# Eleven late tiles' second FFNs held back instead of eight, and the products of the last norms on VectorE

## The chip, the cores and the metric

One core of one Trainium2 chip. The metric is device time in microseconds (us) of one launch. In the text, TensorE is the matmul engine (PE in the profile, PEld its weight loads), VectorE is DVE, ScalarE is ACT, GpSimd is POOL, and SP is the engine that issues nearly all DMAs. Each engine runs its instructions in the order in which the program gives them; semaphores hold an instruction until what it needs is there.

## The reference: what is computed

The input x has 4 batches of 4096 rows of 512 numbers (f32). One block of a network is computed:

```
x = x + 0.5 * ffn(layernorm(x))
x = x + attention(layernorm(x))        # 16 heads of 32, each row sees 13 neighbours
x = x + 0.5 * ffn(layernorm(x))        # the same weights as above
```

`ffn` is one 512 x 512 matrix product in which both sides are first quantised in blocks of 32 numbers: block maximum of the absolute values divided by 7.5 is the scale, the quotient is rounded to a grid of 6-bit floats, and the result is multiplied back. The attention is local: 13 neighbours with a bias for each relative position, softmax, then a 512 x 512 projection.

## The kernel before

**Tiles and precision.** The 16384 rows are 128 tiles (NT) of 128 rows. All large products are made of f16 high and low halves: `product` (L146) issues twelve matmuls of 128x128 on 128x512 (low by high, high by low, high by high, over four chunks of 512), all recorded on L151. A tile needs six such products in some form: the first FFN, the values, its share of the q and k projections (made for four tiles together, two products for each of four chunks of heads), the output projection and the second FFN.

**The schedule.** The work is software-pipelined by hand. `begin(slot, stage, rank)` (L162) puts a generator into a numbered slot; `run_slot` (L165) runs the stages of a slot by rank, and a stage that yields `(n, rank)` goes on n slots later with that rank. The order in which the slots emit instructions is the order on each engine. A tile, and an item of attention (one chunk of four heads for four tiles; there are 128 items m), takes STEP = 7 slots. For tile t with k = 7t: load at k - 18, first norm at k - 10, first FFN at k + 5, values at k + 20, output projection at `out_slot(t)`, usually k + 93, second FFN at `second_slot(t)`, usually 12 slots after the output projection. For item m with k = 7m: q and k projections at k + 38 and k + 39, scores (`softmax`, line L442 on TensorE, into `ps`) at k + 42, probabilities by values (`attend`, L512, into `pv`) at k + 59.

**A quantised norm.** `quantised_norms(slot)` (L220) makes the quantised input of an FFN, for all tiles that `enlist` put into this slot. In the middle of the kernel these are two: the third norm n3 of tile t (before its second FFN), and the first norm n1 of tile t + 15, because 7t + 95 is the slot of both; each instruction then works on 1024 columns. Its stages, mostly one slot apart: `factors` (L183; GpSimd: variance to reciprocal root, L186, L189, L192), normalising (ScalarE, L233), block maxima, scale and reciprocal (VectorE, L239, L240, L244), product with the reciprocal (GpSimd, L246), rounding to fp8 (ScalarE, L249), product with the scale (GpSimd, L251), high half (ScalarE, `high`, L200), low half (VectorE, `low`, L204) and the DMA transpose by SP (L205) into `xT`, the left side of the FFN. The fp8 tile has one buffer (pool `q8p`, L99), as has the f16 tile of the halves (pool `hlp`, L100). `spare` (L227) is true when the first tile of a norm is 123 or later; then y and the halves lie in buffers of the pool `xp` (L96, 23 buffers, which hold the rows of the tiles in flight).

**Between scores and scores.** For item m: VectorE adds the bias and the two parts of the scores (L467, L470) and takes the maximum `top` (L474); GpSimd subtracts it (L476); ScalarE takes exp (L478); VectorE sums and inverts (`total`, L481 to L483); GpSimd multiplies (L485); ScalarE makes the f16 copies (L489, L490); GpSimd the low part (L492); SP transposes p (L494). The q and k of the next item are evacuated between: high halves by ScalarE (L373), low halves by VectorE (L377); the scores of the item wait for the second low half. `ring` (L539 and L545) holds the attention's output.

**The end.** Tiles 113 to 120 are `HELD` (L582): their second FFN waits for the end of the pipeline. Their `xT` takes a buffer of `xp`. `second_slot` (L595) spreads them over slots 932 to 946, among the output projections of 121 and 122 and the last `attend`s (pv 125 at slot 934, pv 126 at 941, pv 127 at 948). Then come the output projections of 123 to 127 (slots 951 to 959), the second FFNs of 121 and 122 (960, 961) and of 123 to 127 (963 to 971). The values of the last group of items are brought back from DRAM as stacks (L418), issued by SP among its transposes and stores (L564). The bias of a second FFN is added on GpSimd (L573).

The lines that place the held tiles:

```
HELD = range(NT - 15, NT - 7)
...
if t in HELD:
    return (n_items - 1) * STEP + PV - (16, 13, 10, 6, 5, 4, 3, 2)[t - HELD[0]]
if i in (-2, -1):
    return out_slot(NT - 1) + 3 + i
return out_slot(t) + F2
```

Of the kernel before, what the change touches and what calls it, by code (L numbers as in the profile page):

```python
# [27 lines left out]
F16 = mybir.dt.float16  # L28
# [4 lines left out]
ALU = mybir.AluOpType  # L33
# [4 lines left out]
P = 128  # L38
# [7 lines left out]
GROUP = 4  # L46
# [4 lines left out]
QB = 32  # L51
# [13 lines left out]
def macaron_kernel(  # L65
# [12 lines left out]
    nc = tc.nc  # L78
# [3 lines left out]
    KC = dim // P  # L82
# [3 lines left out]
    NT = n_batch * length // P  # L86
# [15 lines left out]
    x2p = ctx.enter_context(tc.tile_pool(name="x2p", bufs=2))  # L102
# [26 lines left out]
    def bc(t, n):  # L129

        return t.unsqueeze(2).to_broadcast([t.shape[0], t.shape[1], n])
# [14 lines left out]
    def product(pm, lhs, rhs):  # L146

        n = 0
        for a, b in ((0, 1), (1, 0), (0, 0)):
            for c in range(KC):  # L150
                nc.tensor.matmul(  # L151
                    pm, lhs(a, c), rhs(b, c), start=(n == 0), stop=(n == 3 * KC - 1)
                )
                n += 1
# [7 lines left out]
    def begin(slot, stage, rank=5):  # L162
        slots.setdefault(slot, []).append((rank, stage))
# [19 lines left out]
    def factors(t, which, mv, n=1):  # L183

        rs = sm.tile([P, n], F32, tag=f"rs{which}{n}", name=f"rs{which}_{t}")
        nc.gpsimd.tensor_scalar(  # L186
            rs, mv[:, :n, 1], XS ** -2, LN_EPS * XS ** -2, ALU.mult, ALU.add
        )
        nc.gpsimd.tensor_tensor(rs, rs, minus_half[:, :n], ALU.pow)  # L189
        nb = sm.tile([P, n], F32, tag=f"nb{which}{n}", name=f"nb{which}_{t}")  # L190
        if n == 1:
            nc.gpsimd.tensor_scalar(nb, mv[:, 0, 0:1], rs, -1.0, ALU.mult, ALU.mult)  # L192
        else:
            nc.gpsimd.tensor_tensor(nb, mv[:, :n, 0], rs, ALU.mult)
            nc.gpsimd.tensor_scalar(nb, nb, -1.0, None, ALU.mult)
        return rs, nb

    def high(y, hl):

        nc.scalar.copy(hl[:, :, 0, :], y)  # L200

    def low(y, hl, dst):

        nc.vector.tensor_tensor(hl[:, :, 1, :], y, hl[:, :, 0, :], ALU.subtract)  # L204
        nc.sync.dma_start_transpose(out=dst, in_=hl.rearrange("p u s k -> p (u s k)"))  # L205

    together = {}

    def enlist(slot, t, which):
        together.setdefault(slot, ([], []))[0].append((t, which))

    def moments(slot, t, which):
        tiles, mv = together[slot]
        if not mv:
            mv.append(sm.tile([P, 2, 2], F32, tag="mv", bufs=4, name=f"mv{slot}"))
        statistics(t, which, mv[0][:, tiles.index((t, which)), :])

    def quantised_norms(slot):  # L220

        tiles, mv = together.pop(slot)
        n = len(tiles)
        rs, nb = factors(slot, "q", mv[0], n)
        yield 1, 1

        spare = tiles[0][0] >= NT - GROUP - 1  # L227
        if spare:
            y = xp.tile([P, dim], F32, tag="x", name=f"yq{slot}").unsqueeze(1)
        else:  # L230
            y = yp.tile([P, 2, dim], F32, tag="yq", bufs=2, name=f"yq{slot}")[:, :n]
        for u, (t, _) in enumerate(tiles):
            nc.scalar.activation(  # L233
                y[:, u], xs[t], AF.Identity, bias=nb[:, u : u + 1], scale=rs[:, u : u + 1]
            )
        yield 1, 1
        yb = y.rearrange("p u (n q) -> p (u n) q", q=QB)
        sc = sm.tile([P, 2 * NB], F32, tag="sc", bufs=4, name=f"sc{slot}")[:, : n * NB]
        nc.vector.tensor_reduce(sc, yb, AX.X, ALU.max, apply_absolute_value=True)  # L239
        nc.vector.scalar_tensor_tensor(  # L240
            sc, sc, F8_SCALE / Q_MAX, least[:, : n * NB], ALU.mult, ALU.max
        )
        r = sm.tile([P, 2 * NB], F32, tag="r", bufs=4, name=f"r{slot}")[:, : n * NB]
        nc.vector.reciprocal(r, sc)  # L244
        yield 1, 1
        nc.gpsimd.tensor_tensor(yb, yb, bc(r, QB), ALU.mult)  # L246
        yield 1, 1
        q8 = q8p.tile([P, 2, dim], F8, tag="q8", name=f"q8_{slot}")[:, :n]
        nc.scalar.activation(q8, y, AF.Identity, bias=nudge, saturate=False)  # L249
        yield 1, 3  # L250
        nc.gpsimd.tensor_tensor(  # L251
            yb, q8.rearrange("p u (n q) -> p (u n) q", q=QB), bc(sc, QB), ALU.mult
        )
        yield 1, 3
        if spare:
            hl = xp.tile([P, dim], F32, tag="x", name=f"hlq{slot}").bitcast(F16)
            hl = hl.rearrange("p (u s k) -> p u s k", u=1, s=2)
        else:
            hl = hlp.tile([P, 2, 2, dim], F16, tag="hlq", name=f"hlq{slot}")[:, :n]
        high(y, hl)  # L260
        yield 1, 1
        if tiles[0][0] in HELD and tiles[0][1] == "n3":
            xT = xp.tile([P, dim], F32, tag="x", name=f"xT{slot}").bitcast(F16)
            xT = xT.rearrange("p (u s c q) -> p u s c q", u=1, s=2, c=KC)
        else:
            xT = xtp.tile([P, 2, 2, KC, P], F16, tag="xT", name=f"xT{slot}")
        low(y, hl, xT[:, :n].rearrange("p u s c q -> p (u s c) q"))
        for u, (t, _) in enumerate(tiles):
            ys[t] = xT[:, u]
# [11 lines left out]
    def first_half(t):  # L281

        yield from ffn(t, "f1")
        yield 1, 2
        mv = sm.tile([P, 1, 2], F32, tag="mvn2", name=f"mvn2_{t}")
        statistics(t, "n2", mv[:, 0, :])
        yield 1, 2
        rs, nb = factors(t, "n2", mv)
        yield 1, 2
        y = yp.tile([P, 1, dim], F32, tag="yn2", bufs=1, name=f"yn2_{t}")  # L290
        nc.scalar.activation(y[:, 0], xs[t], AF.Identity, bias=nb, scale=rs)
        hl = hlp.tile([P, 1, 2, dim], F16, tag="hln2", name=f"hln2_{t}")
        high(y, hl)
        yield 2, 2
        g, i = divmod(t, GROUP)
        if i == 0:
            x2[g] = x2p.tile([P, 2, KC, GROUP, P], F16, tag="x2", name=f"x2_{g}")
        low(y, hl, x2[g][:, :, :, i, :].rearrange("p s c q -> p (s c) q"))

    x2 = {}  # L300
# [44 lines left out]
    n_items = n_batch * NG * KC  # L345
# [204 lines left out]
    def project_out(t, slot):  # L550

        r = t * P % RING
        pm = ps_m.tile([P, dim], F32, tag="mm", name=f"pmo_{t}")
        product(
            pm, lambda s, c: ring[:, s, c, r : r + P], lambda s, c: wt[:, s, c, PO : PO + dim]
        )
        yield 1, 8
        nc.vector.scalar_tensor_tensor(xs[t], pm, cp, xs[t], ALU.mult, ALU.add)
        moments(slot, t, "n3")

    def second_half(t):

        yield from ffn(t, "f2")
        nc.sync.dma_start(out=of[t * P : (t + 1) * P, :], in_=xs.pop(t))  # L564
# [3 lines left out]
    STEP = 7  # L568

    F1, V, QK, SC, PV, OUT, F2 = 5, 2 * STEP + 6, 5 * STEP + 3, 6 * STEP, 8 * STEP + 3, 13 * STEP + 2, 12  # L570
# [4 lines left out]
    def one(f, *args):  # L575
        f(*args)
        return
        yield

    HELD = range(NT - 15, NT - 7)  # L582
    LAST = NT - GROUP - 1

    def out_slot(t):


        i = t - LAST
        if i >= 0:
            return (n_items - 1) * STEP + PV + 3 + 2 * i  # L590
        if i >= 1 - GROUP:
            return LAST * STEP + PV + 21 + 4 * i
        return t * STEP + OUT

    def second_slot(t):  # L595

        i = t - LAST
        if t in HELD:
            return (n_items - 1) * STEP + PV - (16, 13, 10, 6, 5, 4, 3, 2)[t - HELD[0]]
        if i in (-2, -1):  # L600
            return out_slot(NT - 1) + 3 + i
        return out_slot(t) + F2

    for t in range(NT):
        k = t * STEP
        begin(k - 18, one(load, t), 0)
        enlist(k - 10, t, "n1")
        if not 0 < t < EARLY:
            begin(k - 11, one(moments, k - 10, t, "n1"), 1)
        begin(k + F1, first_half(t))  # L610
        begin(k + V, values(t))
        begin(k + F1, one(add_bias, t, half_ffn_b), 8)
        at = out_slot(t)
        begin(at - 5, one(add_bias, t, after_b), 8)
        enlist(at + 2, t, "n3")
        begin(at, project_out(t, at + 2))
        begin(at + 6 if t < LAST else second_slot(t) - 2, one(add_bias, t, half_ffn_b), 8)
        begin(second_slot(t), second_half(t))
    for slot in together:
# [7 lines left out]
    for n in range(n_batch * NG):  # L627
        k = n * GROUP * STEP
        b, g = divmod(n, NG)
# [4 lines left out]
    with tc.tile_pool(name="setup", bufs=1) as sp, tc.tile_pool(name="scratch", bufs=2) as scr:  # L634
# [18 lines left out]
        for _ in quantised_norms(-10):  # L653
            pass
        chunks = (8, 9, 10, 11, 12, 13, 14, 15, 0, 4, 1, 5, 2, 6, 3, 7)
        for o in chunks:
            w, i = (qkv_w, o) if o < 3 * KC else (proj_w, o - 3 * KC)
# [266 lines left out]
```

## Time and profile before

| what | us |
|---|---|
| median of three runs (2367.25 to 2368.54) | 2367.49 |
| the profiled execution, its own time | 2366.79 |
| its span, first to last instruction | 2365.0 |
| TensorE busy | 2273.6 (96%) |
| VectorE busy | 2022.5 (86%) |
| GpSimd busy | 1987.6 (84%) |
| ScalarE busy | 1326.8 (56%) |
| mean granted TensorE clock | 0.994 |
| start of the scores of item 118 | 2155.39 |
| start of the scores of item 122 | 2223.16 |
| start of the scores of item 127, the last | 2286.48 |
| end of the output projection of tile 123 | 2325.45 |
| end of TensorE's last product | 2361.04 |

How to read it: times inside the execution are counted from the start of the span. A line of the timeline gives start, duration, engine, line of the kernel, operation, what it writes and reads, the shapes and a count of merged instructions; in brackets stand the time for which the engine was idle before it and what ended that. Matmuls overlap: twelve of one product show as 2.75 us, but the next product starts 2.59 us after the first. A table by windows gives the busy time of each engine in a stretch, the granted clock (1.00 is full speed), the share of the DMA engines and GB/s.

### The profile page before, as it was taken

Reading aid. Unit: us, or ns where it says so; the run is one execution under the profiler, and the core shown is the slowest. Engines: PE = TensorE matmul, PEld = TensorE weight load, DVE = VectorE, ACT = ScalarE, POOL = GpSimd, SP = SyncE. Lnnn points to the kernel's source line nnn. Section 1 sums busy time; section 2 is a strip of 40 time slices with the busy share of each in tenths; the row PEclk is TensorE's granted clock in tenths of the full one; section 3 lists DMA queues with packets and bytes.
Section 4 is the critical chain, followed back from the end, with each engine's and each line's share of the span. In section 5 each row is a group of like instructions: output and inputs, shape, how many; then the busy total and the mean of one; then the engine's idle time right before and its main releaser. Section 6 shows DMA issues by size and latency. Waiting matters only on the chain.

```text
span 2365.0 us, 82328 instructions
## 1 busy us (share of the span) xinstructions
PE 2273.6 (96%) x35539; PEld 1115.4 (47%) x35539; DVE 2022.5 (86%) x3588; ACT 1326.8 (56%) x2080; POOL 1987.6 (84%) x2012
## 2 busy tenths in 40 slices
PE   0799999999999999999999999999999999999988
PEld 0255444444444444444444444444444444444543
DVE  8799888888888888888888888888888888888785
ACT  4466556555555555555555565555555555555542
POOL 5588888888888888888888888888888888888886
PEclk9899999999999999999999999999999999999999
DMA  5789787787777777777777778777777778677763
GB/s 154 146 168 165 156 160 155 147 159 156 151 157 152 156 158 153 156 152 158 153 157 153 153 159 154 153 154 156 158 151 160 151 152 160 153 152 155 133 121 104
DMA packets 925701, 360.59 MB, mean 152 GB/s; under 512 B 718876, under 2 KB 889752, under 8 KB 925336
## 3 DMA queue, kind: packets, MB, share of 16 engines
q1 hardware_dynamic: 924992, 354.79, 73.3%
q8 instruction: 278, 4.55, 0.9%
q10 hardware_dynamic: 344, 0.53, 0.1%
q14 instruction: 87, 0.71, 0.1%
HBM read 110.15 MB, written 67.29 MB: 75 GB/s over the span
## 4 chain that ended last, share of the span: by engine, by line
PE 94%; DVE 3%; DMA 1%; POOL 1%; issue 1%; ACT 0%; SPq 0%; DVEq 0%; ACTq 0%; POOLq 0%
PE pmqk L151 28%; PE pmf L151 27%; PE pmo L151 14%; PE pmv L151 14%; PE ps L442 7%; PE pv L512 3%; DVE fw L761 0%; DMA xT<-hlq 0%; DMA fw<-in_L_ffn_weight_dram 0%; DVE stn L180 0%; DVE wq L763 0%; DVE hlq L204 0%; DVE wqh L757 0%; DMA rows<-in_L_attn_qkv_w_dram 0%; DVE whl L791 0%
## 5 line engine op out<-in xcount | busy, mean ns | idle before, releaser
L151 PE MATMUL pmf<-wt,xT 128*128 128x512 f16 x3048 | 703.5, 381 | 9.1 <-DMA xT<-hlq 9.1
L151 PE MATMUL pmqk<-x,wt 128*128 128x512 f16 x3072 | 705.7, 379 | 1.4 <-DVE vt L315 1.4
L151 PEld LDWEIGHTS <-xT 128*128 128x128 f16 x3048 | 299.1, 98 | 373.7 <-DMA xT<-hlq 11.5
L151 PEld LDWEIGHTS <-wt 128*128 128x128 f16 x3072 | 289.6, 98 | 336.6 <-issue 1.9
L151 PE MATMUL pmv<-wt,x 128*128 128x512 f16 x1536 | 355.0, 381 | 5.1 <-DVE mvn L181 5.1
L246 POOL TENSOR_TENSOR yq<-yq,r 128x1024 f32<-128x1024 f32 (+1 forms) x141 | 246.5, 1748 | 130.0 <-DVE r L244 130.0
L151 PE MATMUL pmo<-wt,ring 128*128 128x512 f16 x1536 | 354.8, 381 | 0.8 <-issue 0.8
L573 POOL TENSOR_TENSOR x<-x,half_ffn_b 128x512 f32<-128x512 f32 x256 | 327.4, 1279 | 0.1
L279 DVE SCALAR_TENSOR_TENSOR x<-pmf,coef,x 128x512 f32<-128x512 f32 x256 | 179.7, 702 | 156.4 <-PE pmf L151 155.9
L314 ACT CAST vt<-pmv 128x512 f16<-128x512 f32 x128 | 74.9, 585 | 388.9 <-PE pmv L151 388.9
L539 ACT ACTIVATE ring<-pv 128x510 f16<-128x510 f32 (+8 forms) x224 | 82.3, 414 | 368.4 <-PE pv L512 368.4
L180 DVE BATCH_NORM_STATS2 stn<-x 128x6 f32<-128x512 f32 x384 | 265.3, 691 | 8.9 <-DMA x<-in_L_attn_x_dram 0.2
L251 POOL TENSOR_TENSOR yq<-q,sc 128x1024 f32<-128x1024 fp8e4 (+1 forms) x141 | 246.7, 1749 | 0.0
L151 PEld LDWEIGHTS <-x 128*128 128x128 f16 x1536 | 150.8, 98 | 188.1 <-DMA x<-hln 5.6
L377 DVE SCALAR_TENSOR_TENSOR qk<-pmqk,qk_b,qk 128x512 f16<-128x512 f32 x256 | 190.5, 744 | 42.2 <-ACT qk L373 41.1
L151 PEld LDWEIGHTS <-ring 128*128 128x128 f16 x1536 | 140.7, 98 | 159.4 <-issue 3.3
L249 ACT ACTIVATE q<-yq,nudge 128x1024 fp8e4<-128x1024 f32 (+1 forms) x141 | 149.9, 1063 | 114.3 <-POOL yq L246 106.1
L485 POOL TENSOR_TENSOR sf<-sf,total 128x714 f32<-128x714 f32 (+2 forms) x128 | 178.6, 1395 | 34.5 <-ACT yq L233 19.1
L373 ACT ACTIVATE qk<-pmqk,qk_b 128x512 f16<-128x512 f32 x256 | 176.1, 688 | 52.1 <-PE pmqk L151 50.8
L186 POOL TENSOR_SCALAR rsq<-mv 128x2 f32<-128x2 f32 (+1 forms) x141 | 130.1, 923 | 89.3 <-DVE mv L181 86.6
L233 ACT ACTIVATE yq<-x,nbq,rsq 128x512 f32<-128x512 f32 x254 | 193.0, 804 | 18.0 <-POOL nbq L192 17.5
L492 POOL TENSOR_TENSOR p<-sf,p 128x714 f16<-128x714 f32 (+2 forms) x128 | 192.6, 1504 | 0.0
(145 smaller groups left out, 3459.7 us busy)
## 6 DMA issues: line engine op xcount, KB each, us to landing
vs<-vd SPq DMA_DIRECT2D x144, 357.0 KB
x<-in_L_attn_x_dram SPq DMA_DIRECT2D x128, 256.0 KB
vd<-vt SPq DMA_DIRECT2D x128, 256.0 KB
out_dram<-x SPq DMA_DIRECT2D x128, 256.0 KB
vs<-vd SPq DMA_DIRECT2D x24, 378.0 KB
vs<-vd SPq DMA_DIRECT2D x24, 315.0 KB
rows<-in_L_attn_qkv_w_dram SPq DMA_DIRECT2D x12, 256.0 KB
xT<-hlq SPq DMA_TRANSPOSE x141
```

The source lines that it names most:

```text
L151: nc.tensor.matmul(pm, lhs(a, c), rhs(b, c), start=(n == 0), stop=(n == 3 * KC - 1))
L180: nc.vector.bn_stats(st, xs[t])
L233: nc.scalar.activation(y[:, u], xs[t], AF.Identity, bias=nb[:, u : u + 1], scale=rs[:, u : u + 1])
L246: nc.gpsimd.tensor_tensor(yb, yb, bc(r, QB), ALU.mult)
L251: nc.gpsimd.tensor_tensor(yb, q8.rearrange("p u (n q) -> p (u n) q", q=QB), bc(sc, QB), ALU.mult)
L279: nc.vector.scalar_tensor_tensor(xs[t], pm, cf, xs[t], ALU.mult, ALU.add)
L373: nc.scalar.activation(t[:, s, 0, KN:], pms[s], AF.Identity, bias=bias)
L377: nc.vector.scalar_tensor_tensor(t[:, s, 1, KN:], pms[s], bias, t[:, s, 0, KN:], ALU.add, ALU.subtract)
L442: nc.tensor.matmul(ps[rows, u, :sides, w * KN : (w + 1) * KN], t[rows, 0, part, q0 : q0 + QR], t[rows, 1, :sides, k0 : k0 + KN], start=par ...
L485: nc.gpsimd.tensor_tensor(s, s, bc(total[:, :n], KN), ALU.mult)
L492: nc.gpsimd.tensor_tensor(p[:, :n, KN : 2 * KN], s, ph, ALU.subtract)
L573: nc.gpsimd.tensor_tensor(xs[t], xs[t], b, ALU.add)
```

## The change

Tiles 110 to 120 are held instead of 113 to 120. The second FFNs of 110 to 119 go to slots 932 to 946, that of 120 to slot 966, between those of 124 (965) and 125 (967). The norm n3 of every held tile is enlisted one slot later than before, at three slots after the output projection instead of two; so the n3 of 110, 111 and 112 no longer falls into the slot of the n1 of 125, 126 and 127. The transposed inputs of the held tiles 115 to 120 lie in buffers of the pool `x2p`, those of 110 to 114 in `xp`. Where `spare` is true, the two products of a quantised norm run on VectorE.

```diff
+    held = []
     together = {}
...
-        nc.gpsimd.tensor_tensor(yb, yb, bc(r, QB), ALU.mult)
+        mult = nc.vector if spare else nc.gpsimd
+        mult.tensor_tensor(yb, yb, bc(r, QB), ALU.mult)
         yield 1, 1
         q8 = q8p.tile([P, 2, dim], F8, tag="q8", name=f"q8_{slot}")[:, :n]
         nc.scalar.activation(q8, y, AF.Identity, bias=nudge, saturate=False)
         yield 1, 3
-        nc.gpsimd.tensor_tensor(
+        mult.tensor_tensor(
             yb, q8.rearrange("p u (n q) -> p (u n) q", q=QB), bc(sc, QB), ALU.mult
         )
...
-        if tiles[0][0] in HELD and tiles[0][1] == "n3":
+        t0 = tiles[0][0]
+        is_held = t0 in HELD and tiles[0][1] == "n3"
+        if is_held and t0 >= NT - 13:
+            g, i = divmod(t0 - (NT - 13), GROUP)
+            if i == 0:
+                held.append(x2p.tile([P, 2, KC, GROUP, P], F16, tag="x2", name=f"held{g}"))
+            xT = held[g][:, :, :, i, :].unsqueeze(1)
+        elif is_held:
             xT = xp.tile([P, dim], F32, tag="x", name=f"xT{slot}").bitcast(F16)
...
-    HELD = range(NT - 15, NT - 7)
+    HELD = range(NT - 18, NT - 7)
...
+        if t == HELD[-1]:
+            return out_slot(NT - 1) + 7
         if t in HELD:
-            return (n_items - 1) * STEP + PV - (16, 13, 10, 6, 5, 4, 3, 2)[t - HELD[0]]
+            return (n_items - 1) * STEP + PV - (16, 13, 10, 9, 8, 6, 5, 4, 3, 2)[t - HELD[0]]
...
-        enlist(at + 2, t, "n3")
-        begin(at, project_out(t, at + 2))
+        n3 = at + (3 if t in HELD else 2)
+        enlist(n3, t, "n3")
+        begin(at, project_out(t, n3))
```

## The prediction

> **What bounds it.** I read the page first: TensorE has 96% of the span and 94% of the chain. So a second FFN that leaves the middle is worth its length there, if TensorE still sets the pace and if the end has a hole for it. The busy times, cut at the starts of the scores of items 118 to 122, test the first:
>
> ```profile
> core 0: us, PE busy (x) PEld busy (x) DVE busy (x) ACT busy (x) POOL busy (x), PEclk, DMA share, GB/s
> ...
> 2155.39:2172.98 17.59, 17.59 (x278) 8.63 (x277) 15.09 (x26) 10.10 (x16) 15.23 (x16) 1.00 0.87 153
> 2172.98:2190.57 17.59, 17.59 (x278) 8.66 (x277) 15.10 (x26) 10.08 (x16) 15.21 (x16) 1.00 0.68 142
> 2190.57:2208.16 17.59, 17.59 (x278) 8.67 (x277) 13.44 (x24) 10.05 (x17) 15.68 (x17) 1.00 0.81 150
> 2208.16:2223.16 15.00, 15.00 (x267) 7.49 (x266) 12.03 (x23) 5.87 (x10) 10.20 (x12) 1.00 0.75 129
> ```
>
> A step is 17.59 us of TensorE without a gap; without a second FFN it is 15.00, so one product of twelve matmuls costs 2.59. VectorE and GpSimd have 15.1 and 15.2 us in the same step: more than the 15.00 that is left when an FFN goes. Then TensorE's timeline from 2250 us on, for the holes (time waited in brackets):
>
> ```profile
> 2260.07 1.34 PE L442 MATMUL ps<-qk 32*32 32x84 f16 x144 [2.14 <-DVE qk L377]
> ...
> 2272.20 1.34 PE L442 MATMUL ps<-qk 32*32 32x84 f16 x144 [2.15 <-DVE qk L377]
> 2273.48 4.42 PE L151 MATMUL pmo<-wt,ring 128*128 128x512 f16 x12
> ...
> 2306.32 0.83 PE L512 MATMUL pv<-pT,vs 126*32 126x30 f16 x72 [4.67 <-DMA vs<-vd]
> 2307.08 15.04 PE L151 MATMUL pmf<-wt,xT 128*128 128x512 f16 x60
> ...
> 2341.41 2.76 PE L151 MATMUL pmf<-wt,xT 128*128 128x512 f16 x12 [0.39 <-DMA xT<-hlq]
> 2346.10 2.76 PE L151 MATMUL pmf<-wt,xT 128*128 128x512 f16 x12 [1.93 <-DMA xT<-hlq]
> 2351.39 9.63 PE L151 MATMUL pmf<-wt,xT 128*128 128x512 f16 x36 [2.53 <-DMA xT<-hlq]
> ```
>
> 13.8 us of holes, of two kinds. Before the scores of 125 and 126 TensorE waits for VectorE's low half of qk; held work that comes later cannot fill that. The stack load (4.67) and the last tiles' transposes (4.85) leave holes that it can. Three groups also run long at a lower granted clock: 4.42 against 2.76; 15.04 against 13.1 (5 x 2.59 and the last one's tail); 9.63 against 7.9: 5.3 us more.
>
> **Moved out of the middle.** The FFNs of 110, 111 and 112 leave the steps to scores 119, 120 and 121: 3 x 2.59 = **-7.78**, if nothing else is late there.
>
> **What their norms do.** Held norms begin one slot later, so 110 to 112 no longer pair with the first norms of 125 to 127. These become single, and the test `spare` (first tile 123 or later) holds for them as well: eight norms, not five, move their products to VectorE. Per step VectorE has 15.10 - 0.70 (one residual, L279) + 0.7 (absmax, scale and reciprocal of 1024 columns, 1.75, become two of 512, 2.44) + 0.1 (low halves, 1.21 to 2 x 0.67) + two products. Such a product is a f32 tensor_tensor of 512 columns with a broadcast factor; the set-up has it, at both its prices:
>
> ```profile
> 25.20 1.52 DVE L762 TENSOR_TENSOR wq<-fw,w_r 128x512 f32<-128x512 f32 x1
> ...
> 42.85 0.67 DVE L762 TENSOR_TENSOR wq<-fw,w_r 128x512 f32<-128x512 f32 x1
> ```
>
> At 25.2 GpSimd ran a product of its own (24.64 to 30.5 almost without a break), at 42.85 none. So 0.67 to 1.53 each, and VectorE has 16.5 to 18.3 us for a step of 15.00. GpSimd loses 2 x 1.91, gets 2 x 1.05 and 0.2 of factors: 13.7.
>
> The Trainium skill, "GPSIMD Engine Reference", section 1, says that GpSimd's SBUF interfaces are shared with VectorE where a VectorE instruction has two SBUF inputs. The two rows above agree. Its section 4.1 advises VectorE for such products; by 0.67 against 1.05 alone this change would win 0.38 a product, which leaves out who else needs VectorE then.
>
> There is a wait as well. The fp8 tile (L99) has one buffer, so ScalarE's rounding of 110 waits for VectorE's second product of 125, queued behind `top`. Behind that rounding wait GpSimd's second product, p's low half, and the next subtraction of `top`; behind these exp, total and the next low half of qk, which the scores need. Once round by the rows: subtraction 1.39, exp 0.90, total 1.34, qk 0.74, two absmax groups 2.44, first FFN's residual 0.70, product 0.67, moments 0.87, values' low half 0.68, bias, sum and top 2.68, product 0.67, rounding 0.72, GpSimd's product 1.05, p's low half 1.50 = 16.4 us, against 15.00. The subtraction for 118 moves from 2159.96 to 59.5 (end of `top`) + 0.67 + 0.72 + 1.05 + 1.50 = 2163.5 and ends at 2164.9; the next two end 16.4 and some 1.0 of contention (half of what all of it would cost) apart, at 2182.3 and 2199.6. Exp, total and qk, with one low half of 0.6 between, take 3.6 more: scores 119 stay in time (2168.5 against 2170.4), 120 start at 2186.0 instead of 2185.4 and 121 at 2203.1 instead of 2200.4. **+2.7**; ends +0.2 (no contention, every wait hidden) and +4.5 (contended products, 18.5 a turn). By scores 122 the load (12.0) has let VectorE catch up.
>
> **One slot later for every held norm.** This hits the later steps, where nothing stands between the second qk product and the scores. VectorE's timeline before scores 126:
>
> ```profile
> 2266.11 0.67 DVE L204 TENSOR_TENSOR hlq<-yq,hlq 128x512 f16<-128x512 f32 x1
> 2268.72 0.75 DVE L377 SCALAR_TENSOR_TENSOR qk<-pmqk,qk_b,qk 128x512 f16<-128x512 f32 x1 [1.93 <-ACT qk L373]
> 2269.39 0.74 DVE L545 SCALAR_TENSOR_TENSOR ring<-pv,ring 128x12 f16<-128x12 f32 x2
> 2270.05 0.93 DVE L481 TENSOR_REDUCE total<-sf 128x18 f32<-128x756 f32 x1
> ```
>
> Now the norm's low half (L204) runs ahead of an idle 1.93 us. With the later slot its rank puts it between `ring` and `total`, and ScalarE's cast of the high half (0.62, 0.54 from start to start) between its `ring` and its first qk half. Both are inside the chain to the second low half of qk: 0.54 + 0.60 = 1.14 a step. Scores 125 and 126 pay all of it. 123, 124 and 127 had 0.35, 0.48 and 0.32 us between the end of the low half and their start, and pay 0.79, 0.66 and 0.82. Sum **+4.5**; ends +1.9 (ScalarE's part hidden) and +8 (the low halves beside GpSimd: 1.51 and 1.92 are rows of L204).
>
> The holes before 125 and 126 grow to 3.3 us. The trace has half clock after 2.15 (+1.66 on L151) and none after 2.14. One more such spell is about even: **+0.8**, ends -1.7 and +1.7. The skill's "TensorE: Matmul & The Clock Gate", part 1, has half rate follow an idle window of some 3.4 us, free-running; by that no hole of 3.3 would throttle and this term would be -1.7, but the row shows it after 2.15, and the row decides.
>
> Scores 127, at 2286.48 now: -7.78 + 2.7 + 4.5 + 0.8 = **+0.2**. The steady gain is given back before the tail begins.
>
> **The tail.** Now it is 2361.04 - 2286.48 = 74.6 us to the end of TensorE. After: scores 1.28, three pv 1.95, and up to the FFN of 122 nineteen products instead of seventeen, 49.3: 52.5 us. Two more FFNs (5.2) stand ahead of pv 126, whose stack came 4.67 late; its last load is now also issued ahead of a transpose (1.28 on SP). So that hole and its slow spell close. The output product of 123 ends at 1.28 + 1.95 + 13 x 2.59 = 37.0.
>
> From there the last five tiles, in VectorE's order, with 1.62 for a residual with moments, 1.07 for an absmax group, 0.67 for products and low halves: low half 123 ends at 13.6, and with 2.75 for the transpose its FFN starts at 16.4 (now 16.0: GpSimd leaves the chain, but VectorE's queue takes its place). Low half 124 ends at 18.7, FFN at 21.5; 125, 126, 127 land by 25.2, 27.0 and 30.9, FFN 120 fills the wait before 125, and TensorE ends at 34.5. But GpSimd's five bias adds (1.27 each), no longer spread between products, run at 17 to 24 in one piece beside VectorE's products. At 1.4 each (L204 has 1.41 to 1.50 there) FFN 124 starts at 23.1 after a 4 us hole, with a slow spell, and the end is 37.7. I take 36.6, nearer the contended rows. VectorE's in-order residual of 120 ahead of low half 127 costs nothing: 30.9 or 34.1 against 127's turn at 31.9 or 35.1. Three later stores and SP's 0.37 each are hidden by TensorE's queue.
>
> Tail 37.0 + 36.6 = 73.6 against 74.6: **-1.0** (ends -3.1 and +0.1).
>
> **Sum.** -7.78 + 2.7 + 4.5 + 0.8 - 1.0 = **-0.7 us**. The profiled execution took 2366.79 (span 2365.0 and 1.79 around it); that becomes 2366.1, and with the median 0.70 above it **2366.8**.
>
> **Rivals.**
> - *The waits stay hidden.* The split steps keep up (+0.2), half of the 1.14 disappears (+2.3), no further slow spell, tail -1.5: -6.8, so 2360.7. For it: the edits fill real holes, and a low half beside idle GpSimd is 0.67. Against: VectorE's 16.5 us in 15.00.
> - *VectorE beside GpSimd sets the pace.* Its place is the three split steps and the chain to scores 123 to 127: 4.5 from 18.5 us turns, 6.5 from low halves of 1.5, 1.7 of clock, tail 0: +4.9, so 2372.4. It decides once late steps and slow spells cost more than 8.8 together, the gain with my tail. For it: 1.22 is the mean of the 28 low halves of single norms. Against: GpSimd waits for `total` (1.04 to 1.82 us) about when they would run.
> - *It doesn't do as told.* Slots count 23 of 23 x buffers in use while held tiles wait; if one is late, a first norm or a held transpose stalls: above 2373.
>
> **Chances.** Likeliest case, within 0.2% (4.7 us, about what a measurement of this kernel tells from no change): 0.57. Waits hidden and below that: 0.24. Slower by more: 0.16 for VectorE's pace, 0.03 for buffers. The range leaves out 0.1 on each side: with the ends of the terms, but not all on one side, 2361.0 to 2373.0.
>
> **What would show it.** Scores 118 to 122 about 15.0, 15.6, 17.1 and 15.0 us apart; holes ahead of scores 123 to 127 of 0.8, 0.7, 3.3, 3.3 and 0.8; L204 just before `total`; no hole at pv 126; FFN 120 between 124 and 125; VectorE without long idle times while the last five norms run. Wrong: scores 121 near 2200.4, or holes of 2.1 still.

## The result: 0.43% slower

The changed kernel takes 2378.45 us (median of four runs, 2377.54 to 2380.88), the kernel before 2367.95 on the same chip: a ratio of 1.0043, 95% interval 1.0028 to 1.0058. I had forecast 2366.8 and a range from 2361.0 to 2373.0. The profiled execution took 2377.54 us with a span of 2375.7.

I cut the execution at the starts of the scores of items 118, 122 and 127, as before. Up to scores 118 the two agree within 0.02 us (2155.39 and 2155.41).

| us | before | after | forecast | measured difference |
|---|---|---|---|---|
| scores 118 to 122 (three FFNs gone, norms split) | 67.77 | 69.52 | -5.1 | +1.75 |
| scores 122 to 127 (norms one slot later) | 63.32 | 69.54 | +5.3 | +6.22 |
| scores 127 to the end of TensorE | 74.56 | 77.50 | -1.0 | +2.94 |

The busy times of the engines of the kernel after, in the four steps from scores 118 to 122 (columns as in the prediction):

```profile
2155.41:2171.72 16.31, 15.07 (x266) 7.57 (x265) 15.16 (x22) 9.05 (x15) 11.82 (x15) 1.00 0.66 118
2171.72:2191.32 19.60, 15.22 (x264) 7.55 (x264) 18.90 (x32) 10.36 (x17) 14.32 (x18) 0.99 0.74 136
2191.32:2209.93 18.61, 16.50 (x264) 8.30 (x264) 17.15 (x30) 9.56 (x17) 13.61 (x15) 0.92 0.48 96
2209.93:2224.93 15.00, 15.00 (x266) 7.45 (x265) 14.12 (x25) 8.24 (x13) 13.26 (x15) 1.00 0.92 155
```

TensorE's work did fall from 17.59 to 15.07 and 15.22 us in the first two steps, so the FFNs are gone; the third has 16.50 because its granted clock fell to 0.92. But the second step is 19.60 long, and VectorE is busy for 18.90 of it. How much of that is work and how much is waiting for GpSimd, the next section shows. TensorE's timeline of the kernel after shows the holes:

```profile
2171.72 1.28 PE L451 MATMUL ps<-qk 32*32 32x84 f16 x136 [1.24 <-DVE qk L386]
2191.32 1.97 PE L451 MATMUL ps<-qk 32*32 32x84 f16 x136 [2.38 <-DVE qk L386]
2209.93 1.28 PE L451 MATMUL ps<-qk 32*32 32x84 f16 x136 [1.40 <-DVE qk L386]
...
2264.53 1.49 PE L451 MATMUL ps<-qk 32*32 32x84 f16 x144 [3.27 <-DVE qk L386]
2265.95 4.45 PE L151 MATMUL pmo<-wt,ring 128*128 128x512 f16 x12
...
2279.59 1.97 PE L451 MATMUL ps<-qk 32*32 32x84 f16 x144 [3.27 <-DVE qk L386]
...
2314.74 0.79 PE L521 MATMUL pv<-pT,vs 126*32 126x30 f16 x72
...
2348.99 2.76 PE L151 MATMUL pmf<-wt,xT 128*128 128x512 f16 x12 [1.51 <-DVE sc L240]
2356.10 5.30 PE L151 MATMUL pmf<-wt,xT 128*128 128x512 f16 x12 [4.34 <-DVE sc L240]
```

The scores wait for VectorE's low half of qk. The three steps with split norms have holes before the scores and, not shown, the second and the third also before the values (2.00 and 0.71 us). Scores 125 and 126 wait 3.27 instead of 2.14 and 2.15. The hole of 4.67 before pv 126 (2314.74) is gone, as forecast; instead the FFN of 124 waits 4.34 and then runs at a granted clock of 0.50. The last two brackets name L240, VectorE's block scale of a later norm, which no FFN reads; the same hole in n1_gpsimd reads `4.36 <-DMA xT<-hlq`. So FFN 124 waits for its transpose, which SP issues behind VectorE's low half. The cause of the 3.27 stands in VectorE's timeline of the kernel after, before scores 126:

```profile
2275.50 0.75 DVE L386 SCALAR_TENSOR_TENSOR qk<-pmqk,qk_b,qk 128x512 f16<-128x512 f32 x1 [3.28 <-ACT qk L382]
...
2276.82 0.68 DVE L204 TENSOR_TENSOR hlq<-yq,hlq 128x512 f16<-128x512 f32 x1
2277.42 0.93 DVE L490 TENSOR_REDUCE total<-sf 128x18 f32<-128x756 f32 x1
```

The norm's low half (L204) stands right ahead of `total`, and the idle time before the qk half has grown from 1.93 to 3.28: the low half no longer fills it, and ScalarE's cast delays the high half that ends it. This is the mechanism that was forecast.

### The profile page after: what moved, and what is told of

It is laid out like the page before. It is cut to its first block, busy times and chain, and to the rows that moved or that the text cites. A ratio compares the mean times of both kernels' runs of the same rounds, so it can differ in the third digit from the quotient of the medians.

```text
span 2375.7 us, 82380 instructions
## 1 busy us (share of the span) xinstructions
PE 2276.0 (96%) x35539; PEld 1117.3 (47%) x35539; DVE 2038.8 (86%) x3616; ACT 1327.7 (56%) x2086; POOL 1974.7 (83%) x2008
## 4 chain that ended last, share of the span: by engine, by line
PE 92%; DVE 5%; issue 1%; ACT 1%; DMA 1%; POOL 0%; SPq 0%; DVEq 0%; ACTq 0%; POOLq 0%
PE pmqk L151 27%; PE pmf L151 27%; PE pmo L151 14%; PE pmv L151 13%; PE ps L451 7%; PE pv L521 3%; DVE hlq L204 1%; DVE stn L180 0%; DVE sc L240 0%; DVE qk L386 0%; DVE fw L773 0%; DVE total L490 0%; DMA fw<-in_L_ffn_weight_dram 0%; DVE x L288 0%; DMA rows<-in_L_attn_qkv_w_dram 0%
## 5 line engine op out<-in xcount | busy, mean ns | idle before, releaser
L151 PE MATMUL pmf<-wt,xT 128*128 128x512 f16 x2976 | 686.0, 381 | 10.1 <-DVE sc L240 5.9
L151 PEld LDWEIGHTS <-xT 128*128 128x128 f16 x2976 | 291.8, 98 | 365.0 <-DMA xT<-hlq 12.0
L248 POOL TENSOR_TENSOR yq<-yq,r 128x1024 f32<-128x1024 f32 (+1 forms) x136 | 238.5, 1754 | 134.5 <-DVE r L245 132.3
L253 POOL TENSOR_TENSOR yq<-q,sc 128x1024 f32<-128x1024 fp8e4 (+1 forms) x136 | 237.8, 1748 | 8.0 <-ACT q L251 8.0
```

Of the source, the lines that this page charges most:

```text
L151: nc.tensor.matmul(pm, lhs(a, c), rhs(b, c), start=(n == 0), stop=(n == 3 * KC - 1))
L248: mult.tensor_tensor(yb, yb, bc(r, QB), ALU.mult)
L253: mult.tensor_tensor(yb, q8.rearrange("p u (n q) -> p (u n) q", q=QB), bc(sc, QB), ALU.mult)
```

## What happens in a split step

Timelines of ScalarE, GpSimd and VectorE of the kernel after, in the first split step. ScalarE:

```profile
2160.24 0.72 ACT L251 ACTIVATE q<-yq,nudge 128x512 fp8e4<-128x512 f32 x1 [3.71 <-DVE yq L253]
...
2165.36 0.89 ACT L487 ACTIVATE sf<-sf,coef 128x714 f32<-128x714 f32 x1 [0.71 <-POOL sf L485]
```

GpSimd:

```profile
2161.03 1.04 POOL L253 TENSOR_TENSOR yq<-q,sc 128x512 f32<-128x512 fp8e4 x1 [3.66 <-ACT q L251]
2162.04 1.49 POOL L501 TENSOR_TENSOR p<-sf,p 128x714 f16<-128x714 f32 x1
2163.49 1.84 POOL L485 TENSOR_TENSOR sf<-sf,top 128x714 f32<-128x714 f32 x1
...
2166.88 1.27 POOL L582 TENSOR_TENSOR x<-x,after_b 128x512 f32<-128x512 f32 x1
```

VectorE:

```profile
2162.87 1.21 DVE L204 TENSOR_TENSOR hlq<-yq,hlq 128x512 f16<-128x512 f32 x1 [0.33 <-ACT hlq L200]
2164.00 1.87 DVE L204 TENSOR_TENSOR hln<-yn,hln 128x512 f16<-128x512 f32 x1
...
2167.05 1.64 DVE L204 TENSOR_TENSOR hlq<-yq,hlq 128x512 f16<-128x512 f32 x1
2168.62 0.88 DVE L490 TENSOR_REDUCE total<-sf 128x17 f32<-128x714 f32 x1
...
2169.84 1.17 DVE L492 TENSOR_TENSOR total<-total,p_scale 128x17 f32<-128x17 f32 x1
...
2174.44 0.63 DVE L248 TENSOR_TENSOR yq<-yq,r 128x512 f32<-128x512 f32 x1
```

ScalarE's rounding of the held tile waits 3.71 us for VectorE's second product, because the fp8 tile has one buffer. GpSimd waits for that rounding, and its product, p's low half and the subtraction of `top` come late and in one piece. The subtraction starts at 2163.49, which the forecast had as 2163.5. But they now run exactly when VectorE has its low halves, and the two engines take turns: GpSimd's p ends at 2162.04 + 1.49 = 2163.53, and the low half begun at 2162.87 ends 0.55 later, at 2164.08; the subtraction ends at 2165.33, and the next low half ends 0.54 later, at 2165.87. The third low half, begun at 2167.05 beside a bias addition of GpSimd (2166.88 to 2168.15), ends 0.54 after that. Alone a low half takes 0.67. The four instructions L204 (three) and L492 last 5.89 us together instead of 3 x 0.67 + 0.18 = 2.19: 3.7 us of waiting for GpSimd in VectorE's queue. Some 0.6 of it was there before the change, where the same step's product of `total` (L483) took 0.79 us beside a bias addition. The products that the change moved onto VectorE were themselves not hindered (0.63 and 0.68). From one subtraction to the next it is 19.60 us (2163.49, 2183.09, 2202.67).

The Trainium skill, "SBUF — State Buffer", section "Who interferes with whom", says that a VectorE instruction with two SBUF inputs contends with a GpSimd instruction that reads SBUF, and that the port they share is an exclusive lock. The trace agrees: the three low halves end 0.55, 0.54 and 0.54 us after GpSimd's instruction, however long they had waited. I had priced this as a fixed, longer duration instead.

## The experiments

The stages of all kernels, each from its one profiled execution. Each ratio is to runs of the kernel before on the same chip (their medians are 2367.30 to 2367.95 us):

| kernel | 118 to 122 | 122 to 127 | 127 to end | median us | ratio to before, 95% interval |
|---|---|---|---|---|---|
| before | 67.77 | 63.32 | 74.56 | | |
| after | 69.52 | 69.54 | 77.50 | 2378.45 | 1.0043 (1.0028 to 1.0058) |
| hold_only | 66.46 | 70.23 | 72.19 | 2370.28 | 1.0013 (1.0004 to 1.0023) |
| products_only | 67.76 | 64.95 | 77.92 | 2371.77 | 1.0018 (1.0009 to 1.0027) |
| n1_gpsimd | 66.46 | 70.17 | 77.49 | 2374.98 | 1.0028 (1.0017 to 1.0040) |
| slot2 | 69.50 | 65.07 | 79.12 | 2373.48 | 1.0026 (1.0015 to 1.0038) |
| own_fp8 | 64.13 | 69.04 | 77.46 | 2372.64 | 1.0021 (1.0011 to 1.0030) |
| own_fp8_gp | 61.96 | 69.61 | 70.33 | 2364.22 | 0.9986 (0.9977 to 0.9995) |
| no_late_bias | 69.51 | 69.21 | 74.59 | 2375.75 | 1.0028 (1.0018 to 1.0039) |
| later_slot_only | 67.76 | 68.98 | 69.89 | 2369.09 | 1.0006 (0.9997 to 1.0015) |
| one_late_only | 67.75 | 63.12 | 70.44 | 2364.78 | 0.9986 (0.9977 to 0.9995) |
| pair_kept | 60.80 | 63.43 | 73.69 | 2360.45 | 0.9969 (0.9956 to 0.9981) |
| pair_two_late | 60.83 | 63.43 | 71.47 | 2358.32 | 0.9959 (0.9946 to 0.9971) |

**hold_only**: the change with all products on GpSimd.

```diff
-        mult = nc.vector if spare else nc.gpsimd
+        mult = nc.gpsimd
```

> The change with all products back on GpSimd: eleven held tiles and their later slot alone. Theory A (the wait for VectorE's products of the three split norms makes the split steps long): scores 122 start near 2218 instead of 2224.9, the later steps keep their 6.2 us, the tail falls to about 72 us from scores 127: about 2366. Rival B (splitting the paired norms costs this much whoever makes the products): scores 122 still near 2225, and with the shorter tail about 2373.

Neither theory was right alone. Scores 118 to 122 took 66.46 us, 6.5 more than four steps of 15.0 and 3.1 less than after. So splitting the norms costs 6.5 even with GpSimd's products, and VectorE's products add 3.1. The tail is 5.3 us shorter than after. The whole, 2370.28, lies between the two forecasts.

**products_only**: before, with the products of the last five norms on VectorE.

```diff
-        nc.gpsimd.tensor_tensor(yb, yb, bc(r, QB), ALU.mult)
+        mult = nc.vector if spare else nc.gpsimd
+        mult.tensor_tensor(yb, yb, bc(r, QB), ALU.mult)
...
-        nc.gpsimd.tensor_tensor(
+        mult.tensor_tensor(
```

> The kernel before with the products of the last five norms on VectorE and nothing else. Theory A (VectorE's own queue and the bias adds beside it make the tail longer): the middle as before, from the output product of 123 to the end 38 to 40 us instead of 35.6: 2370 to 2372. Rival (the products are shorter on VectorE and the tail's loss in the change comes from FFN 120): 33 to 35 us, 2366 to 2367.

Theory A held: from the output product of 123 to the end it is 39.1 us. The move alone costs 3.4 us in the tail (77.92 against 74.56): FFN 124 waits 4.26 us, at half clock afterwards. The second of the diff's two ideas is a loss by itself.

**n1_gpsimd**: the change, with the products of the first norms of 125 to 127 on GpSimd and only those of the last five on VectorE.

```diff
-        mult = nc.vector if spare else nc.gpsimd
+        mult = nc.vector if spare and tiles[0][1] == "n3" else nc.gpsimd
```

> The change, but the products of the first norms of 125 to 127 stay on GpSimd; only the last five norms have theirs on VectorE. Theory A: scores 122 as in the run with all products on GpSimd, near 2218, the tail as in the change (77.5 us from scores 127): about 2371. Rival B: scores 122 near 2225 and 2378, as in the change.

Stages one and two are those of hold_only, the tail that of after. So theory A holds for where the time goes, but its numbers do not: scores 122 start at 2221.95 and the whole is 2375, since hold_only itself came 4 us above what theory A had for it. The two places where VectorE got products are independent: 3.1 us in the split steps, 5.3 in the tail.

**slot2**: the change, with the later slot only for 110 to 112.

```diff
-        n3 = at + (3 if t in HELD else 2)
+        n3 = at + (3 if t in HELD[:3] else 2)
```

> The change, but the third norms of 113 to 120 keep their old slot; only those of 110 to 112 begin a slot later. Theory A (the later slot puts high and low halves into the chain to the scores): scores 122 as in the change, holes before scores 125 and 126 back at 2.1, scores 122 to 127 61.6 to 63.3 us apart instead of 69.5: about 2372. Rival (the later steps are long because VectorE is still behind): 69 us and 2378.

Scores 122 to 127 fell by 4.5 us, the holes before 125 and 126 were 2.15 again. In these steps the later slot's price is as forecast. The stage, 65.07, is still above theory A's 61.6 to 63.3, since both holes have a slow spell behind them, where before had one. And the tail is 1.6 us longer than after, with new holes of 0.68 and 0.52 us before two held FFNs, put down to VectorE's residuals; why, no run shows. So the profiled execution gains 2.9 us, not 4.5.

**own_fp8**: the change, with a buffer of its own for the fp8 tile of the single norms on VectorE.

```diff
-        q8 = q8p.tile([P, 2, dim], F8, tag="q8", name=f"q8_{slot}")[:, :n]
+        if spare:
+            q8 = yp.tile([P, 2, dim], F32, tag="yq", bufs=2, name=f"q8_{slot}")
+            q8 = q8[:, 0].bitcast(F8)[:, :dim].unsqueeze(1)
+        else:
+            q8 = q8p.tile([P, 2, dim], F8, tag="q8", name=f"q8_{slot}")[:, :n]
```

> The change, but the rounded fp8 values of the single norms on VectorE go into a buffer of the pool of the paired norms' y, so that the held tile's rounding no longer waits for VectorE's second product. Theory A, the wait for the one fp8 tile sets the turn of the split steps: from scores 118 to scores 122 drops from 69.5 us to 65 or less, ScalarE's idle time of 3.7 before its second rounding is gone, and the whole is 2373 to 2375. Theory B, VectorE's longer queue beside GpSimd (low halves of 1.2 to 1.9, total times scale at 1.2) sets it: 68.5 to 70, the wait shows up behind another instruction, 2377 to 2379. The tail should not change in either (77.5).

Theory A held: 64.13 instead of 69.52. ScalarE's and GpSimd's timelines of own_fp8 in the first split step, against those of after above:

```profile
2156.60 0.72 ACT L255 ACTIVATE q<-yq,nudge 128x512 fp8e4<-128x512 f32 x1
```

```profile
2157.51 1.05 POOL L257 TENSOR_TENSOR yq<-q,sc 128x512 f32<-128x512 fp8e4 x1
...
2159.97 1.84 POOL L489 TENSOR_TENSOR sf<-sf,top 128x714 f32<-128x714 f32 x1
```

The rounding has no wait, and the subtraction starts 4.39 us after scores 118 (2159.97 - 2155.58) instead of 8.08. The whole was a little better than expected. The 5.4 us are the price of one buffer. Of the 9.5 over four steps of 15.0, 4.1 stay: the step to scores 121 is 18.09 long.

**own_fp8_gp**: both, an own fp8 buffer and GpSimd's products.

```diff
-        mult = nc.vector if spare else nc.gpsimd
+        mult = nc.gpsimd
```

> The change with all products on GpSimd and the fp8 tile of the single norms in a buffer of its own: both prices of the split steps but the larger number of instructions taken away. Theory A, the single fp8 tile is what the split costs: from scores 118 to 122 61 to 62.5 us (66.5 with one fp8 tile and GpSimd's products, 64.1 with an own tile and VectorE's), the whole about 2365 to 2366. Theory B, with GpSimd's products the split costs by its extra instructions and transposes, and the wait was hidden behind them: 64 or more, 2368 to 2370.

Theory A again: 61.96. The four cases of scores 118 to 122 (60.0 would be free of waits):

| us | one fp8 tile | own fp8 tile |
|---|---|---|
| products on VectorE | 69.52 | 64.13 |
| products on GpSimd | 66.46 | 61.96 |

The buffer is worth 4.5 to 5.4, the engine 2.2 to 3.1. The whole fell more than expected, since the tail gained from the buffer too (70.33 against 72.19 of hold_only): ScalarE's roundings no longer wait there for the product before, and the hole of 2.01 us before FFN 124 is gone.

**no_late_bias**: the change without the last bias of tiles 123 to 127.

```diff
-        begin(at + 6 if t < LAST else second_slot(t) - 2, one(add_bias, t, half_ffn_b), 8)
+        if t < LAST:
+            begin(at + 6, one(add_bias, t, half_ffn_b), 8)
```

> The change, but the bias of the second FFN is not added to tiles 123 to 127 (five GpSimd additions less; these tiles' rows lack that bias). Theory A, the additions, which now run on GpSimd in one piece, slow VectorE's two-input operations beside them: f124's hole of 4.3 us falls to about 2 and its slow clock goes, from the scores of 127 to the end 73 to 75 us instead of 77.5, the whole about 2375. Theory B, VectorE's own queue (ten more products of 0.67 in the chain of five norms) sets the end even beside an idle GpSimd: 76.5 to 77.5, about 2378.

The tail falls to 74.59, theory A, though a part of the slow clock stays. In the kernel after, VectorE's timeline of the tail has

```profile
2349.95 1.56 DVE L248 TENSOR_TENSOR yq<-yq,r 128x512 f32<-128x512 f32 x1
2351.44 1.75 DVE L204 TENSOR_TENSOR hlq<-yq,hlq 128x512 f16<-128x512 f32 x1
2353.11 1.74 DVE L253 TENSOR_TENSOR yq<-q,sc 128x512 f32<-128x512 fp8e4 x1
```

beside GpSimd's five additions in one piece:

```profile
2349.70 7.50 POOL L582 TENSOR_TENSOR x<-x,half_ffn_b 128x512 f32<-128x512 f32 x5
```

Each of the two engines waits for the other's instruction in turn. Without the additions the same instruction of VectorE in no_late_bias is short:

```profile
2351.25 0.68 DVE L248 TENSOR_TENSOR yq<-yq,r 128x512 f32<-128x512 f32 x1
```

and FFN 124 waits 2.42 us instead of 4.34:

```profile
2355.45 4.45 PE L151 MATMUL pmf<-wt,xT 128*128 128x512 f16 x12 [2.42 <-DMA xT<-hlq]
```

So of the 5.3 us that VectorE's products cost in the tail, 2.9 go with the additions beside them. The other 2.4 were not taken apart; VectorE's own longer queue and the slow spell that stays are the likely parts.

**later_slot_only**: before, with the later slot for the eight held norms.

```diff
-        enlist(at + 2, t, "n3")
-        begin(at, project_out(t, at + 2))
+        n3 = at + (3 if t in HELD else 2)
+        enlist(n3, t, "n3")
+        begin(at, project_out(t, n3))
```

> Before, with the third norm of the eight held tiles begun one slot later and nothing else. Theory A, the low half ahead of total and the cast ahead of the first half of qk lengthen each of the steps to scores 123 to 127: holes of 0.6, 0.6, 3.3, 3.3 and 0.8 us there, 4.5 us more (and up to 1.7 of slow clock): 2372 to 2374. Rival, that these holes come from the change's fuller queues: holes of 2.15 before 125 and 126 only, within 1 us of before.

The holes are those of theory A, but the whole missed its range, at 2369.09. TensorE's timeline of later_slot_only:

```profile
2263.38 1.51 PE L442 MATMUL ps<-qk 32*32 32x84 f16 x144 [3.27 <-DVE qk L377]
...
2309.27 0.79 PE L512 MATMUL pv<-pT,vs 126*32 126x30 f16 x72 [1.19 <-DMA vs<-vd]
```

The steps lose 5.7 us, but the hole before pv 126 shrinks from 4.67 to 1.19 and its slow spell goes, for the stack's load came only some 2 us later (pv 126 starts 2.2 us later than before, counted from scores 118). In the kernel after, that hole is already filled with FFNs, and the steps' loss isn't won back there.

**one_late_only**: before, with the second FFN of 120 at slot 966.

```diff
+        if t == HELD[-1]:
+            return out_slot(NT - 1) + 7
         if t in HELD:
```

> Before, with one edit: the second FFN of 120 goes to slot 966, between those of 124 and 125. If the last tiles' transposes have room for it, the hole of 2.5 us before 125 to 127 and the slow spell behind it (1.7) go while pv 127 comes 2.6 earlier: 2.5 to 4.2 us less, 2363.5 to 2365.5. Rival, the first norms' wait only moves (its residual on VectorE delays the low halves of 126 and 127): within 1 us of before.

The tail is 4.1 us shorter, the whole 3.1. This edit of the change is good by itself.

**pair_kept**: eleven held, 120 late, but the norms stay paired at the old slot with GpSimd's products; only the transpose of a pair is issued as two.

```diff
-        mult = nc.vector if spare else nc.gpsimd
+        mult = nc.gpsimd
...
+        if is_held and n > 1:
+            nc.vector.tensor_tensor(hl[:, :, 1, :], y, hl[:, :, 0, :], ALU.subtract)
+            dsts = [xT[:, 0], xtp.tile([P, 2, 2, KC, P], F16, tag="xT", name=f"xT{slot}")[:, 0]]
+            for u, (t, _) in enumerate(tiles):
+                nc.sync.dma_start_transpose(
+                    out=dsts[u].rearrange("p s c q -> p (s c) q"),
+                    in_=hl[:, u].rearrange("p s k -> p (s k)"),
+                )
+                ys[t] = dsts[u]
+            return
...
-        n3 = at + (3 if t in HELD else 2)
+        n3 = at + 2
```

> The change without its two costs: eleven tiles held and that of 120 at slot 966 as in the change, but the third norms of 110 to 112 stay paired with the first norms of 125 to 127 (one norm of 1024 columns, of which only the transpose is issued as two, one into the held buffer and one into the usual one), every held norm at its old slot, and all products on GpSimd. My theory, that the split of the pairs (6.5 us), the later slot (4.5), VectorE's products in the split steps (3.1) and in the tail (5.3) are separate prices: scores 122 about 7.8 us earlier than before (near 2215.5), scores 127 near 2279, end about 2.4 us shorter than before: 2357 to 2360. Rival, that in a step without a second FFN VectorE and GpSimd cannot go below some 16.5 us however the norms are grouped: scores 122 near 2221 as with the split on GpSimd, and 2363 to 2366.

Scores 122 come after 60.80 us. TensorE's timeline of pair_kept shows what is left before scores 121 and 126:

```profile
2203.70 1.28 PE L461 MATMUL ps<-qk 32*32 32x84 f16 x136 [0.74 <-DVE qk L396]
...
2268.00 1.58 PE L461 MATMUL ps<-qk 32*32 32x84 f16 x144 [2.15 <-DVE qk L396]
```

The rival is out: a step without an FFN does run in 15.0 us when the norms stay paired. The whole is 2360.45, half a us above my range, 18 us under the kernel after. Against one_late_only the three more held FFNs win 4.3 of their 7.8 us: the tail grows by 3.3, since the hole before pv 126 takes only 4.4 of the 7.8 us of work.

**pair_two_late**: pair_kept, with the second FFN of 119 between those of 123 and 124.

```diff
-        if t == HELD[-1]:
-            return out_slot(NT - 1) + 7
+        if t in HELD[-2:]:
+            return out_slot(NT - 1) + (5, 7)[t - HELD[-2]]
```

> The kernel of pair_kept with the second FFN of 119 moved as well, from slot 946 to 964, between those of 123 and 124, where TensorE still waits 2.02 us for a transpose. If pv 127 can come 2.6 us earlier and the residual of 119 on VectorE doesn't hold up the low half of 124: 1.5 to 2 us less than pair_kept, 2358 to 2359.5. Rival: the wait moves behind 124 or to pv 127, within 0.7 us of pair_kept.

2.2 us are off the tail, a little more than expected: 2358.32, the lowest median of all, and lower than both kernels.

## Why the prediction was wrong, point by point

- **Three FFNs out of the middle, -7.78: right.** The steps of pair_kept are 14.99, 15.00, 15.81 and 15.00 us.
- **The split norms, +2.7: wrong, they cost 9.5** (69.52 against 60.0). This is the step that failed most. Its mechanism, the rounding that waits for VectorE's second product, is what own_fp8 took away, and the first late subtraction came when forecast. The size failed where the text says that the subtractions come "16.4 and some 1.0 of contention (half of what all of it would cost) apart". They came 19.6 apart. The part of the circle from the subtraction over exp and `total` to the second low half of qk was summed as 1.39 + 0.90 + 1.34 + 0.74 = 4.37; it took 8.18 (2163.49 to 2171.67). The subtraction took 0.45 more, the product of `total` 1.0 more (0.6 of that stood already in the kernel before's rows of these steps, which the 1.34 left out), and 2.4 lay between them: exp was done at 2166.25, but `total` began at 2168.62, because VectorE's queue was late by the low halves that had waited for GpSimd and then had a third one to finish. The rest of the circle was summed as 12.0 and took 11.4. I had looked for the contention in the moved products, which had none, and not in the two-input instructions already there. Scores 119, forecast in time, were 1.3 us late for the same reason.
- **The later slot, +4.5: right.** The holes before scores 123 to 127 were forecast as 0.8, 0.7, 3.3, 3.3 and 0.8 and measured as 0.64, 0.63, 3.27, 3.27 and 0.79. slot2 gives 4.5 back in these steps.
- **The clock, +0.8: too low.** One more spell came, as forecast (both 3.27 us holes have one behind them, where before had one behind two holes of 2.15). The holes grew by 4.31 together and the stage by 6.22, which leaves 1.9. In later_slot_only and own_fp8_gp only the second of two such holes had a spell, so this term is partly chance. They lose 5.7 and 6.3 in this stage all the same; their one spell cost 2.6 us, where the two of the kernel after cost 1.8 and 1.4.
- **The tail, -1.0: wrong, it was +2.9.** The filling was right: pv 126 no longer waits, and hold_only's tail is 2.4 us under that of before. What failed is "I take 36.6" for the last five tiles, between 34.5 and 37.7: from the end of the output product of 123 (2331.93) to the end it was 40.0. FFN 124 started 24.2 us in (23.1 in my contended branch), since an instruction beside the additions took 1.56 to 1.75 and not 1.4, and its slow spell cost 2.5 and not 1.7.
- **The rivals.** "VectorE beside GpSimd sets the pace" came nearest, but in part for other reasons. In the split steps the low halves and not the moved products lay beside GpSimd; in the steps to scores 123 to 127, where it expected low halves of 1.5 us, those of the held norms took 0.68. Its price of 2372.4 was 6 us short: it counted the split steps at 4.5 and the tail at 0. The rival with waits hidden was out from the first split step. No wait for an x buffer shows in the split steps.

The errors add up: 6.8 for the split steps, 0.9 for the later ones and 3.9 for the tail, 11.6 of the 11.65 between 2366.8 and 2378.45. What stays open is when a slow clock follows a hole: behind the holes before scores 125 it did in slot2 (2.15 us) and in the kernel after (3.27), and it did not in the kernel before (2.14) or in later_slot_only (3.27).

## What to carry to other kernels

Before work is split into smaller pieces or moved to another engine, look at every single-buffered tile that the pieces share: the second piece waits for the whole chain of the first, with all that is queued behind it. And when a wait moves a block of GpSimd's work, list which two-input VectorE instructions it will then lie beside; price each with the rest of GpSimd's instruction added, not with a longer average. Moving FFNs into the holes of the tail paid most where the norms stayed paired in their old slots (2360.45 and 2358.32). With split norms it took a second fp8 buffer and GpSimd's products to come below before at all (2364.22), and that is no better than moving the FFN of 120 alone (2364.78).

## What the runs showed of the hardware

- Behind the set-up, 25 times in the kernel after, a VectorE tensor_tensor of 128x512 with both inputs in SBUF began while GpSimd ran one of 128x512 or more. Each ended 0.55 us after GpSimd's instruction and lasted 0.72 to 1.94 us, against 0.67 alone. One of 128x17 took 1.17 us beside a bias addition, against 0.18.
- It goes both ways: GpSimd's subtraction took 1.84 instead of 1.39 where a low half was running at its start.
- A hole's length didn't fix what the slow clock behind it cost. Behind holes of 3.27 us before scores 125 it was 1.8 us in the kernel after and nothing in later_slot_only; behind the hole of 2.38 before scores 120 it was 1.3 in the kernel after and nothing in no_late_bias. After the hole of 4.34 us a whole product ran at half clock (5.30 against 2.76).
